# A two-layer metaformer on one core: folds of corners and experts written as additions, and another order of loads at the head of the spectral stage

## The chip, the cores and the metric

The kernel runs on one core of a Trainium2 chip, in float32 throughout. The metric is the device time of one execution in microseconds (us). The engines are named as in the profile: PE (TensorE, matmuls), DVE (VectorE), ACT (ScalarE), POOL (GpSimd), and SP, whose queue issues most DMAs. "L1103" is line 1103 of the kernel before.

## What is computed

The input is 8 images of 128 channels and 32 x 32 tokens. Two layers follow each other:

```
layer 0:  x = x + attention(ln_channels(x))            # 8 heads, all 1024 tokens
          t = t + STU(ln(t))                           # 4 lengths T, T/2, T/4, T/8
   STU:   sum over 16 filters k: causal_conv(phi_k, u) * sigma_k^0.25 @ M_plus_k
          + the same with alternating signs @ M_minus_k, + 3 lags of u @ M_u
layer 1:  x = x + deform(ln_channels(x))               # 3 taps
   deform: offset, mask = convolutions of x with 3 taps, plus their biases
          every tap: 4 bilinear corners (gathered) * weights * mask, @ conv_w
          t = t + experts(ln(t))                       # 8 experts, top 2, gates normalized
   experts: sum over e of gate_e * (t @ expert_w_e) + bias
```

Where the change works, two sums are meant: over 3 taps x 4 corners = 12 gathered rows of 128 channels for each token, added to the token itself; and over 8 experts' gated outputs of 128 channels, added to the token as well.

## The kernel before

**Stages.** Attention runs from the start to about 910 us. Then `spectral_and_second_layer` (from L1533) goes over `work`, 8 images x 16 filters, n = 0 to 127. One n has two halves (`src`), each about 5.19 us of PE: `filter_image` makes the filter's products (p_x, p_y, p_z, L1488) and combines them (ACT L1499 and L1500, POOL's addition L1501, DVE's L1506, L1509, L1516), and `mix` (L1453) multiplies the results of n - 2 with the matrices mf of that filter. `manual_schedule` keeps the order of instructions on each engine as the code writes it.

**The second layer beside it.** While image b is filtered, the second layer of image b - 1 runs in pieces. Two queues of generators, `rows`, are drained by `advance(RATE)`, twice in each half: every `yield` hands back a cost, and pieces are taken until the costs come up to RATE = 3.2 (LAST_RATE = 3.6 while image 7 is filtered, that is for the second layer of image 6). So the costs, which are written by hand, set where an instruction of the second layer stands in its engine's queue. The second layer of image 7 has nothing beside it: from 2558 us it runs alone as the tail (`alone` is true there).

**Corners.** `sampled` (L1052) fetches by 24 indirect DMAs per image (L1077, on POOL), one for each of the NT = 8 groups of 128 tokens and each of 3 taps, into tiles g of 128 x 3 x 4 x 128 (three buffers). ACT scales taps 0 and 1 by the corners' weights (L1095), DVE tap 2 (L1099). Then

```python
nc.vector.tensor_reduce(
    x3[:, i, :], g.rearrange("p t k c -> p c (t k)"), AX.X, ALU.add
)
nc.vector.tensor_add(x3[:, i, :], x3[:, i, :], tok[:, i, :])
```

folds the 12 rows (L1103) and adds the token (L1106). After the eighth group come the statistics (L788, L789), the inverse deviation (L770 to L778; its Newton steps run on POOL while the STU runs, on DVE in the tail), the normalization (L795) and its transposition on PE (p_turn, L919).

**Experts.** For every group PE makes p_e for 4 experts at a time (L1123); ACT gates the first four (L1130), DVE the others (L1135); L1140 folds the 8 rows into a tile `both` by tensor_reduce, and L1143 adds it to x3. PE transposes the sum (p_out, L1155) and it is stored.

**Other work on POOL.** `differences` of the next filter (L1239, L1240), L1501 once per half, and in the first image the sum and difference of the matrices (`terms`, L1371 and L1372).

**The head of the STU.** In this order SP's queue gets: the loads of filters 1 and 2 (`load_filter`, L1257 and L1258, tile teto, three buffers), the four loads of `load_lags` (mu, L1322), the two of `load_parts(0)` (tile m_room, L1366: M_plus and M_minus of filter 0). `prepare(0)` (L1391), an indirect DMA on POOL, is written ahead of them. Once the first half runs, `between` calls `terms` on m_room and loads the next m_room, and in the second half `weigh` (L1379, L1381) makes mf[0], which the first `mix` needs. m_room has one buffer, its tag ("x2") shared with a later tile. Beside it `setup` (from L820) loads the second layer's small weights in pieces, among them the biases of the offsets and masks (L846, L849), zeroes the borders of the tables (L870), and at its end adds the biases to `base` (L906).

Of the kernel before, what the change touches and what calls it, by code (L numbers as in the profile page):

```python
# [11 lines left out]
F32 = mybir.dt.float32  # L12
I32 = mybir.dt.int32
AF = mybir.ActivationFunctionType
ALU = mybir.AluOpType
AX = mybir.AxisListType
PSUM = bass.MemoryType.PSUM

P = 128
B = 8  # L20
C = 128
T = 1024
NT = T // P
# [779 lines left out]
class DeformAndExperts:  # L803
# [17 lines left out]
    def setup(self):  # L821

        nc, cp, ident, dram = self.nc, self.cp, self.ident, self.dram
        (
            conv_w, conv_b, off_w, off_b, mask_w, mask_b, router_w, router_b, expert_w, expert_b
        ) = self.given


        self.gw = cp.tile([C, TAPS * C + TAPS * 9], F32, name="gw")
        nc.sync.dma_start(self.gw[:, 0 : TAPS * C], conv_w.rearrange("c t o -> c (t o)"))  # L830
        off_r = off_w.rearrange("c t (j two) -> c t two j", two=2)
        off_rb = off_b.rearrange("(j two) -> two j", two=2)

        self.base = cp.tile([P, NT, 9], F32, name="base")
        bias = cp.tile([P, 9], F32, name="bias")
        with nc.allow_non_contiguous_dma(reason="small weights"):
            for tap in range(TAPS):
                at = TAPS * C + 9 * tap
                for xy in range(2):
                    nc.sync.dma_start(  # L840
                        self.gw[:, at + 3 * xy : at + 3 * xy + 3], off_r[:, tap, xy, :]
                    )
                nc.sync.dma_start(self.gw[:, at + 6 : at + 9], mask_w[:, tap, :])
                yield
            for xy in range(2):
                nc.sync.dma_start(  # L846
                    bias[:, 3 * xy : 3 * xy + 3], off_rb[xy].partition_broadcast(P)
                )
            nc.sync.dma_start(bias[:, 6:9], mask_b.partition_broadcast(P))  # L849
        yield  # L850
        nc.gpsimd.memset(self.base, 0.0)
        for g in range(4):
            rows = slice(32 * g, 32 * g + 32)
            nc.gpsimd.iota(self.base[rows, :, 0:3], pattern=[[4, NT], [0, 3]], base=g,
                           channel_multiplier=0, allow_small_or_imprecise_dtypes=True)
            nc.gpsimd.iota(self.base[rows, :, 3:6], pattern=[[0, NT], [1, 3]], base=-1,
                           channel_multiplier=1, allow_small_or_imprecise_dtypes=True)

        self.row = cp.tile([P, NT, TAPS], F32, name="row")
        nc.gpsimd.iota(self.row, pattern=[[0, NT], [self.ROWS, TAPS]], base=33,  # L860
                       channel_multiplier=0, allow_small_or_imprecise_dtypes=True)

        zero = cp.tile([33, 4 * C], F32, name="zero")
        nc.gpsimd.memset(zero, 0.0)
        self.tabs = []
        for n in range(2):
            tab = dram.tile([TAPS, self.ROWS, 4, C], F32, name=f"tab{n}")
            for tap in range(TAPS):
                for r0 in (0, T):
                    nc.sync.dma_start(  # L870
                        tab[tap, r0 : r0 + 33].rearrange("r s c -> r (s c)"), zero
                    )
                yield
            self.tabs.append(tab)

        self.shift = [None, ident, None]
        for tap, edge in ((0, 0), (2, 31)):
            s = cp.tile([P, P], F32, name=f"shift{tap}")
            nc.gpsimd.memset(s, 0.0)
            nc.gpsimd.affine_select(  # L880
                out=s, in_=s, pattern=[[-1, P]], base=1 - tap, channel_multiplier=1,
                compare_op=ALU.not_equal, fill=1.0,
            )
            nc.gpsimd.memset(s.rearrange("p (a b) -> p a b", b=32)[:, :, edge : edge + 1], 0.0)
            self.shift[tap] = s
            yield
        self.cb = cp.tile([P, C], F32, name="cb")
        nc.sync.dma_start(self.cb, conv_b.partition_broadcast(P))
        self.rw = cp.tile([C, NE], F32, name="rw")
        nc.sync.dma_start(self.rw, router_w)  # L890
        self.rb = cp.tile([P, NE], F32, name="rb")
        nc.sync.dma_start(self.rb, router_b.partition_broadcast(P))
        yield
        self.ew = cp.tile([C, NE, C], F32, name="ew")
        nc.sync.dma_start(self.ew, expert_w.rearrange("e d c -> d e c"))


        self.ebm = cp.tile([P, NT, C], F32, name="ebm")
        nc.gpsimd.memset(self.ebm, 0.0)
        for i in range(NT):  # L900
            nc.sync.dma_start(self.ebm[i * NE : (i + 1) * NE, i, :], expert_b)
            yield
        self.eidx = cp.tile([P, NT, NE], F32, name="eidx")
        nc.gpsimd.iota(self.eidx, pattern=[[0, NT], [1, NE]], base=0, channel_multiplier=0,
                       allow_small_or_imprecise_dtypes=True)
        nc.vector.tensor_tensor(  # L906
            self.base, self.base, bias.unsqueeze(1).to_broadcast([P, NT, 9]), ALU.add
        )
        yield

# [145 lines left out]
    def sampled(self, b, got, alone):  # L1056
# [3 lines left out]
        nc, sb = self.nc, self.sb  # L1060
        newton = nc.vector if alone else nc.gpsimd
        idx, w, tok = got
        x3 = sb.tile([P, NT, C], F32, tag="x3", name="x3")
# [26 lines left out]
        for i, tap in points:  # L1090
            fetch()
            g = tiles[i]
            if tap < TAPS - 1:
                for k in range(4):
                    nc.scalar.activation(  # L1095
                        g[:, tap, k, :], g[:, tap, k, :], AF.Identity, scale=w[:, i, tap, k : k + 1]
                    )
            else:
                nc.vector.tensor_tensor(  # L1099
                    g[:, tap], g[:, tap], w[:, i, tap, :].unsqueeze(2).to_broadcast([P, 4, C]),  # L1100
                    ALU.mult,
                )
                nc.vector.tensor_reduce(  # L1103
                    x3[:, i, :], g.rearrange("p t k c -> p c (t k)"), AX.X, ALU.add
                )
                nc.vector.tensor_add(x3[:, i, :], x3[:, i, :], tok[:, i, :])  # L1106
            yield 1.7 if alone else 2.6
        tt = sb.tile([P, NT, C], F32, tag="ht", name="tt")
        yield from norm_steps(nc, sb, x3, tt, 1e-5, newton, not alone)
# [8 lines left out]
        for i in range(NT):  # L1118
            g = sb.tile([P, TAPS, 4, C], F32, tag="g", name="ge", bufs=3)
            part = g.rearrange("p t k c -> p (t k) c")[:, 0:NE]  # L1120
            for grp in range(2):
                pe = self.bank("p_e")
                nc.tensor.matmul(  # L1123
                    pe, tc[:, i * P : (i + 1) * P],
                    self.ew[:, grp * 4 : grp * 4 + 4, :].rearrange("d e c -> d (e c)"),
                    start=True, stop=True,
                )
                if grp == 0:
                    for k in range(4):
                        nc.scalar.activation(  # L1130
                            part[:, k], pe[:, k * C : (k + 1) * C], AF.Identity,
                            scale=gate[:, i, k : k + 1],
                        )
                else:
                    nc.vector.tensor_tensor(  # L1135
                        part[:, 4:8], pe.rearrange("p (k c) -> p k c", c=C),
                        gate[:, i, 4:8].unsqueeze(2).to_broadcast([P, 4, C]), ALU.mult,
                    )
                    both = sb.tile([P, C], F32, tag="both", name="both")
                    nc.vector.tensor_reduce(  # L1140
                        both, part.rearrange("p e c -> p c e"), AX.X, ALU.add
                    )
                    nc.vector.tensor_add(x3[:, i, :], x3[:, i, :], both)  # L1143
                yield 1.3 if alone else 2.2
            if i % 4 == 3:
                if not alone:
# [11 lines left out]
                nc.scalar.copy(ot[:, half * 512 : half * 512 + 512], po)  # L1158
                yield
        nc.sync.dma_start(self.out[b].rearrange("c h w -> c (h w)"), ot)  # L1160

    def turn_back(self, src, dst):

# [368 lines left out]

def spectral_and_second_layer(tc, spec, layer, weights):  # L1533
    work = [(b, k) for b in range(B) for k in range(NF)]
    imgs = {0: spec.prepare(0)}
    filters = {0: spec.given.filter, 1: spec.load_filter(1), 2: spec.load_filter(2)}
    less = {0: spec.given.given.diff}
    spec.load_lags()

    mf = {}  # L1540
    parts = spec.load_parts(0)
    both = None

# [44 lines left out]
    for n in range(len(work) + 2):  # L1590
        now = work[n] if n < len(work) else None
        if now is not None:
            b, k = now
            if k == 1 and b + 1 < B:
                starts[b + 1] = spec.begin(b + 1, layer.bank, imgs)
                rows[0].append(starts[b + 1])
            elif k == 0 and b:
                for _ in starts[b]:
                    pass
            us = sums[n] = spec.sb.tile([C, 2, 2, HT], F32, tag="us", name="us", bufs=3)  # L1600
# [128 lines left out]
```

## Time and profile before

| | us |
|---|---|
| median of 3 runs | 2700.72 (2695.61 to 2702.18) |
| the profiled execution | 2699.79 |
| its span (first to last instruction) | 2698.0 |
| busy in it: PE / DVE / POOL / ACT | 2530.0 / 1852.9 / 1448.6 / 1083.5 |
| L1103, 64 folds of corners | 180.4 (2.819 each) |
| L1140, 64 folds of experts | 122.8 (1.919 each) |
| mean granted PE clock | 0.974 of full speed |

A row of the profile gives the line, the engine, the operation, the tiles and shapes, and how often it ran; after the bar come its busy time and the mean of one (in ns), then the idle time of the engine just before it and the instruction that ended that idle time ("<-"). The timeline rows have the start in us, the duration in us and the same names. A row of waits tells who waited for whom: the total in us, how often, and the longest. The 40 digits of a row of slices are the busy tenths of equal parts of the span, 67 us each. In a table of windows the columns are the window, its length, the busy times of PE, PEld (weight loads), DVE, ACT and POOL with the number of instructions, the granted clock, the share of the DMA engines and the GB/s.

### The profile page before, as it was taken

What the parts mean: (1) busy time and instruction counts of PE and PEld (TensorE: products, weight loads), DVE (VectorE), ACT (ScalarE), POOL (GpSimd) and SP (SyncE); (2) the same over time, 40 slices, a digit from 0 to 9 for tenths busy, and PEclk for the clock granted to TensorE, in tenths of its full rate; (3) what the DMA queues carried; (4) which work ended last, traced back from release to release, by engine and by line L of the source; (5) the groups of instructions that cost most, each with busy time, mean ns of one, the idle gap of its engine ahead of it and who ended that gap; (6) DMA issues with size and microseconds to landing.
All of it is one profiled execution on the core that took longest, in us unless ns stands there. A gap on an engine that the chain in (4) does not pass through costs nothing. (4 is left out here: it accounts for less than half of the span.)

```text
span 2698.0 us, 47432 instructions
## 1 busy us (share of the span) xinstructions
PE 2530.0 (94%) x18896; PEld 1769.3 (66%) x18896; DVE 1852.9 (69%) x2728; ACT 1083.5 (40%) x2030; POOL 1448.6 (54%) x1535
## 2 busy tenths in 40 slices
PE   6999999999999799999999999999999999999924
PEld 3555555555555578777787787778778778777712
DVE  3888888888888455448648649648648657658646
ACT  4666766667667111123223224224214224224232
POOL 4777777777788455446246237237236227226230
PEclk9999999999999899999999999999999999999956
DMA  1000000000000254375275266265266266256151
GB/s 29 2 17 2 17 17 2 17 9 10 9 17 17 83 162 153 119 207 160 73 212 169 71 198 184 71 191 176 79 181 194 71 173 194 79 149 202 40 168 35
DMA packets 204675, 267.10 MB, mean 99 GB/s; under 512 B 20308, under 2 KB 138260, under 8 KB 204448
## 3 DMA queue, kind: packets, MB, share of 16 engines
q1 hardware_dynamic: 181312, 205.27, 26.1%
q0 software_dynamic: 16800, 55.59, 6.2%
q10 hardware_dynamic: 6336, 3.15, 0.4%
q8 instruction: 151, 2.47, 0.4%
q14 instruction: 76, 0.62, 0.1%
HBM read 196.02 MB, written 67.92 MB: 98 GB/s over the span
## 5 line engine op out<-in xcount | busy, mean ns | idle before, releaser
L623 POOL TENSOR_TENSOR t<-e 128x1024 f32<-128x1024 f32 x256 | 608.3, 2376 | 199.3 <-ACT e L614 199.0
L651 DVE TENSOR_TENSOR e<-e,rb 128x2048 f32<-128x2048 f32 x256 | 570.8, 2278 | 84.1 <-PE rb L644 84.1
L614 ACT ACTIVATE e<-s 128x2048 f32<-128x2048 f32 x256 | 481.2, 1880 | 253.2 <-PE s L609 250.7
L1501 POOL TENSOR_TENSOR part<-us,part 128x256 f32<-128x256 f32 x256 | 189.9, 743 | 708.5 <-ACT part L1500 707.8
L1453 PE MATMUL po<-us,mf 128*128 128x128 f32 (+2 forms) x2048 | 528.9, 381 | 5.9 <-DVE mf L1381 3.8
L1506 DVE TENSOR_TENSOR part<-p_y,part 128x512 f32<-128x512 f32 x256 | 175.4, 685 | 310.0 <-PE p_y L1488 193.2
L1499 ACT COPY us<-p_x 128x256 f32<-128x256 f32 x256 | 94.8, 370 | 723.2 <-PE p_x L1488 712.8
L1453 PEld LDWEIGHTS po<-us,mf 128*128 128x128 f32 x2048 | 308.2, 191 | 37.5 <-issue 4.8
L609 PE MATMUL s<-q,k 32*128 32x256 f32 x4096 | 296.1, 403 | 14.5 <-ACT e L614 13.7
L661 PE MATMUL av<-e,vt 128*32 128x256 f32 x4096 | 287.9, 388 | 5.3 <-DVE e L651 4.0
L1516 DVE TENSOR_TENSOR us<-p_z,part 128x512 f32<-128x512 f32 x256 | 174.8, 683 | 151.7 <-PE p_z L1488 151.3
L1488 PEld LDWEIGHTS p_z<-diff,gap 128*128 128x128 f32 x1024 | 193.1, 191 | 129.6 <-issue 88.3
L609 PEld LDWEIGHTS s<-q,k 32*128 32x128 f32 x4096 | 186.4, 185 | 137.5 <-ACT e L614 116.3
L1488 PE MATMUL p_z<-diff,gap 128*128 128x256 f32 x1024 | 266.1, 382 | 3.6 <-DVE base L906 3.1
L1095 ACT ACTIVATE g<-g,w 128x128 f32<-128x128 f32 x512 | 161.2, 393 | 118.1 <-DMA g<-tab,here 91.1
L1077 POOL DMA_INDIRECT g<-tab,here x168 | 167.3, 996 | 71.8 <-issue 31.6
L661 PEld LDWEIGHTS av<-e,vt 128*32 128x32 f32 x4096 | 101.3, 109 | 142.2 <-issue 84.3
L1103 DVE TENSOR_REDUCE x<-g 128x128 f32<-128x1536 f32 x64 | 180.4, 2819 | 7.5 <-ACT g L1095 1.5
L1239 POOL TENSOR_TENSOR diff<-teto 128x516 f32<-128x516 f32 x127 | 163.6, 1288 | 1.6 <-DMA teto<-in_phi_o 0.8
L637 DVE RECIPROCAL r<-z 128x256 f32<-128x256 f32 x64 | 112.5, 1757 | 69.5 <-PE z L630 69.3
L1488 PE MATMUL p_y<-diff,gap 128*128 128x256 f32 x512 | 152.6, 379 | 0.1
L1488 PE MATMUL p_z<-teto,ht 128*128 128x256 f32 x512 | 132.3, 381 | 0.0
(264 smaller groups left out, 3731.9 us busy)
## 6 DMA issues: line engine op xcount, KB each, us to landing
mf<-mfd SPq DMA_DIRECT2D x112, 512.0 KB
tab<-gs SPq DMA_DIRECT2D x180, 256.0 KB
teto<-in_phi_o SPq DMA_DIRECT2D x127, 256.5 KB
teto<-in_phi_e SPq DMA_DIRECT2D x127, 256.0 KB
mfd<-mf SPq DMA_DIRECT2D x16, 512.0 KB
xc<-in_x SPq DMA_DIRECT2D x8, 512.0 KB
x1d<-xt SPq DMA_DIRECT2D x8, 512.0 KB
m_room<-in_M_plus SPq DMA_DIRECT2D x16, 256.0 KB
```

Source lines behind the costliest of these rows:

```text
L609: nc.tensor.matmul(s[:, j, c, :], img["k"][rows, hg, 2 * r + c, :], q[rows, qc * QU : (qc + 1) * QU], start=True, stop=True,)
L614: nc.scalar.activation(e.rearrange("p j c q -> p (j c q)"), s.rearrange("p j c q -> p (j c q)"), AF.Exp, scale=float(HD) ** -0.5,)
L623: nc.gpsimd.tensor_add(t, e[:, :, 0, :], e[:, :, 1, :])
L651: nc.vector.tensor_tensor(e, e, un["rb"].unsqueeze(2).to_broadcast([P, NH, 2, QU]), ALU.mult)
L661: nc.tensor.matmul(qrt["av"][32 * j : 32 * j + 32, 0:QU], img["v"][:, 2 * r + c, P * hg + 32 * j : P * hg + 32 * j + 32], un["e", r][:, j, ...
L1077: nc.gpsimd.indirect_dma_start(out=tiles[-1][:, tap].rearrange("p k c -> p (k c)"), out_offset=None, in_=rows, in_offset=bass.IndirectOffs ...
L1103: nc.vector.tensor_reduce(x3[:, i, :], g.rearrange("p t k c -> p c (t k)"), AX.X, ALU.add)
L1453: self.nc.tensor.matmul(out, lhsT, rhs, start=bank not in img["opened"], stop=last, skip_group_check=True)
L1488: nc.tensor.matmul(out, weights, moving, start=start, stop=stop, skip_group_check=True)
L1501: nc.gpsimd.tensor_add(part[:, 0], mine[:, :, 0:P], part[:, 1])
L1506: nc.vector.tensor_tensor(part[:, 2:4], y[:, 0].unsqueeze(1).to_broadcast([C, 2, 2, P]), part[:, 0:2], ALU.add)
L1516: nc.vector.tensor_tensor(result(2, 4), z, part[:, 2:4], ALU.add)
```

## The change

The two folds are written as chains of additions. `add_up(g, (6, 3))` adds rows 6 to 11 of the 12 to rows 0 to 5 (768 elements per partition), then rows 3 to 5 to rows 0 to 2 (384); `three` adds the first of the three left to the token, and the other two to that sum (128 elements each). For the experts `add_up(part, (4, 2))` has 512 and 256 elements, and two additions of 128 go straight into x3; the tile `both` of that place is gone. All their operands are in SBUF. At the head, `load_parts(0)` comes first, then filter 1, `prepare(0)`, `load_lags`, and filter 2. The addition of the biases leaves `setup` for a generator of its own, `settle`, that is queued when filter 1 of image 0 begins; the loads of the biases stay where they were.

```diff
@@ setup
-        nc.vector.tensor_tensor(
-            self.base, self.base, bias.unsqueeze(1).to_broadcast([P, NT, 9]), ALU.add
+        yield
+
+    def settle(self):
+        yield
+        self.nc.vector.tensor_tensor(
+            self.base, self.base, self.bias.unsqueeze(1).to_broadcast([P, NT, 9]), ALU.add
         )
         yield
@@ sampled
-                nc.vector.tensor_reduce(
-                    x3[:, i, :], g.rearrange("p t k c -> p c (t k)"), AX.X, ALU.add
-                )
-                nc.vector.tensor_add(x3[:, i, :], x3[:, i, :], tok[:, i, :])
+                self.add_up(g.rearrange("p t k c -> p (t k) c"), (6, 3))
+                self.three(x3[:, i, :], g[:, 0, 0:3], tok[:, i, :])
...
-                    both = sb.tile([P, C], F32, tag="both", name="both")
-                    nc.vector.tensor_reduce(
-                        both, part.rearrange("p e c -> p c e"), AX.X, ALU.add
-                    )
-                    nc.vector.tensor_add(x3[:, i, :], x3[:, i, :], both)
+                    self.add_up(part, (4, 2))
+                    for k in range(2):
+                        nc.vector.tensor_add(x3[:, i, :], x3[:, i, :], part[:, k])
...
+    def add_up(self, parts, counts):
+        for n in counts:
+            self.nc.vector.tensor_add(parts[:, 0:n], parts[:, 0:n], parts[:, n : 2 * n])
+
+    def three(self, out, parts, more):
+        self.nc.vector.tensor_add(out, parts[:, 0], more)
+        for k in (1, 2):
+            self.nc.vector.tensor_add(out, out, parts[:, k])
@@ spectral_and_second_layer
-    imgs = {0: spec.prepare(0)}
-    filters = {0: spec.given.filter, 1: spec.load_filter(1), 2: spec.load_filter(2)}
-    less = {0: spec.given.given.diff}
-    spec.load_lags()
 
     mf = {}
     parts = spec.load_parts(0)
     both = None
+    filters = {0: spec.given.filter, 1: spec.load_filter(1)}
+    less = {0: spec.given.given.diff}
+    imgs = {0: spec.prepare(0)}
+    spec.load_lags()
+    filters[2] = spec.load_filter(2)
...
                 rows[0].append(starts[b + 1])
+                if b == 0:
+                    rows[0].append(layer.settle())
```

More of the change, by code (lines that the diff above doesn't have):

```diff
@@ L834, in setup @@
         self.base = cp.tile([P, NT, 9], F32, name="base")
-        bias = cp.tile([P, 9], F32, name="bias")
+        bias = self.bias = cp.tile([P, 9], F32, name="bias")
         with nc.allow_non_contiguous_dma(reason="small weights"):
```

## The prediction, on record ahead of the run

> **What bounds the kernel now.** I read the span in slices first, then busy times of single stages, the waits of the STU, and last single rows. The slices (each 67 us):
>
> ```profile
> PE   6999999999999799999999999999999999999924
> DVE  3888888888888455448648649648648657658646
> POOL 4777777777788455446246237237236227226230
> ```
>
> From slice 14 (the STU, 913 to 2558 us) PE is full; DVE and POOL rise together once per image, when the second layer gathers its corners. Only the last two slices leave PE idle. So an edit on DVE pays in three places: the tail, the head, and where DVE holds PE up. One gather stage (image 0's, us; columns PE, PEld, DVE, ACT, POOL):
>
> ```profile
> 1206.00:1257.00 51.00, 50.35 (x237) 40.86 (x237) 46.21 (x52) 23.94 (x81) 38.93 (x43) 1.00 0.65 192
> ```
>
> DVE is busy 46.2 of 51 us. POOL is busy 38.9 in 43 instructions, and the trace shows 0.30 us between its gathers, so it is nearly full as well. Who releases PE, and whom POOL holds up, between 970 and 2560:
>
> ```profile
> PE p_turn L919 <- DVE tt L795: 10.1, 18, 1.0
> PE po L1453 <- DVE us L1516: 2.1, 1, 2.1
> PE p_back L1168 <- DVE x L1530: 1.6, 1, 1.6
> DVE part L1506 <- POOL part L1501: 84.4, 28, 6.2
> ```
>
> PE waits little, but mostly for L795, the normalization that follows the corners. That is where a late fold would come through. Next the rows of the folds and of the one two-input DVE operation beside them:
>
> ```profile
> L1103 DVE TENSOR_REDUCE x<-g 128x128 f32<-128x1536 f32 x64 | 180.4, 2819 | 7.5 <-ACT g L1095 1.5 <-issue 0.5
> L1140 DVE TENSOR_REDUCE both<-ge 128x128 f32<-128x1024 f32 x64 | 122.8, 1919 | 6.2
> L1099 DVE TENSOR_TENSOR g<-g,w 128x512 f32<-128x512 f32 x64 | 54.6, 854 | 14.7 <-DMA g<-tab,cn_idx 12.6 <-DMA g<-tab,here 2.0
> L1106 DVE TENSOR_TENSOR x<-x,tok 128x128 f32<-128x128 f32 x64 | 30.4, 474 | 2.3
> ```
>
> In the tail, alone, L1099 takes 0.69 and L1106 0.29 us: means of 0.854 and 0.474 mean stretching in the STU. Why, at 1233 us:
>
> ```profile
> 1233.61 1.29 POOL L1239 TENSOR_TENSOR diff<-teto 128x516 f32<-128x516 f32 x1
> 1233.73 1.78 DVE L1099 TENSOR_TENSOR g<-g,w 128x512 f32<-128x512 f32 x1 [0.69 <-DMA g<-tab,here]
> 1234.85 1.25 POOL L1240 TENSOR_TENSOR diff<-teto 128x258 f32<-128x258 f32 x1
> ```
>
> L1099 starts beside L1239 and ends about when that has ended plus its own 0.6; then L1240 (0.77 on average) takes 1.25 because it waits for L1099. The two don't overlap. L1103 shows nothing of it: 2.82 on average, 2.75 alone.
>
> [...] the gather issue at 2612.62, inside an L1099, took 1.41 for 0.96. [...] Here, already after the 2.06 us stall at 2479.7, rows of 1.02 took 1.81, 1.91 and 1.23: 1.88 us more.
>
> **The change, part by part.** Prices: 768 elements 0.955, 384 0.555, 512 0.69, 256 0.42, 128 0.29, plus 0.03 for a dependent step, 0.21 for a start-to-start of the last.
>
> *A fold alone.* Corner: 2.79 + 0.21 = 3.00 goes, 0.985 + 0.585 + 0.31 + 0.31 + 0.21 = 2.40 comes: -0.60. Expert: 1.95 + 0.21 = 2.16 goes, 0.72 + 0.45 + 0.31 + 0.21 = 1.69 comes: about -0.45. [...]
>
> *Tail, nothing beside DVE but gathers.* (a) At 2562 DVE works off image 6's last two expert folds before L788 of image 7: -0.9. (b) Corners: DVE's period is 3.79, but POOL issues three gathers at 0.96 + 0.30 each, 3.79 too. A faster DVE gains at most the last fold, -0.6. [...] +2 to +4 over 24 by stepping them through, against 0.6 now. Sum +1.8 (-0.7 to +3). (c) Experts: DVE's period 2.95 (0.69+1.92+0.29 and gaps) is above PE's 2.1, so 8 x -0.45 = -3.6. **Tail -2.7** (-5.1 to -1).
>
> *Head.* SP now issues m_room(0) at 920.3 behind teto1, teto2 and mu; it lands for POOL at 927.21 and PE waits for the first matrices:
>
> ```profile
> 933.92 2.08 PE L1453 MATMUL po<-us,mf 128*128 128x128 f32 x6 [3.80 <-DVE mf L1381]
> 940.91 1.27 POOL L1371 TENSOR_TENSOR both<-m_room 128x512 f32<-128x512 f32 x1 [9.84 <-DMA m_room<-in_M_minus]
> 945.29 1.13 PE L1407 MATMUL p_ut<-flip,ht 128*128 128x128 f32 x8 [2.55 <-DVE us L1509]
> ```
>
> With m_room(0) first on SP (two DMAs ahead of teto1, four mu, teto2's two), terms(0) can start at 922.5 and the 3.80, and about 1.9 of low clock after it, go. But m_room(1) stays behind setup's small loads, at 932.05 on SP, and lands at 940.9; POOL's L1501, DVE's L1509 and PE's p_ut hang on it, and so does a 3.08 wait at 951.6. It moves only if SP starts earlier: 0 to 2.5 us. PE's gain becomes a longer wait at p_ut. teto2 moves behind mu, needed later: nothing. The indirect load of prepare runs on POOL's queue, which is not late: nothing. **Head -1.5** (0 to -3; -15 if every stall and its low clock fell).
>
> *Biases.* The base add (0.22 us of DVE) moves from setup's end to filter 1; its loads stay. First use is more than 100 us later. 0, at most +0.2 if DVE isn't hidden.
>
> *Expert folds in the STU, images 0 to 6.* DVE has slack and PE doesn't wait for them, except at 2356 (1.58 for L1530, and 1.7 of low clock): -1 (0 to -3). L1143 shows only 0.08 of stretch.
>
> *Corner folds in the STU.* This decides. In image 0's stage (50 us) POOL's three additions take 6.5 + 4.3 + 7.3 = 18.1 us. DVE's locking instructions now cover 8 x 0.98 = 7.8 us, 16% of it, so 0.16 x 18.1 = 2.9 us should be waited: measured 2.2 here and, over the 56 folds of the STU, (54.6 + 30.4 - 64 x 0.98)/56 = 0.40 each, 3.2 an image. The rule holds. After, they cover 8 x (0.69 + 0.08 + 2.40) = 25.4 us, 51%: 9.2 us waited, 6 to 7 more, against a saving of 8 x 0.60 = 4.8. So +1.2 to +2.2, and more because gathers fall into the lock too: I take +2.5 an image (-1 to +6). After the last fold DVE runs back to back through L788/L789 into L770, POOL's Newton steps and L795, for which PE already waits; later passes through in full, earlier gains only those 10.1 us in seven images at most. A wait of 1.4 + 2.5 comes near the stall that halved the clock: I add 1.0 (0 to 1.9). **Six images x 3.5 = +21.** Image 6 advances faster (3.6 for 3.2) and DVE is 8 us behind already, with the 2.06 + 1.88 stall: contention and saving there, 0 (-3.9 to +6).
>
> **Sum**: -2.7 - 1.5 - 1 + 21 + 0 = +16 on the profiled execution's 2699.8 us (span 2698.0, 1.8 around it; 0.9 below the median 2700.72). That gives 2716, +0.6%.
>
> **Rivals.** *Savings win (faster).* The lock costs less than the additions save. Place: the corner stages. Price: contention stays under 4.8 us an image more, i.e. under 3.2 + 4.8 = 8 of the 18.1 us wait (44% instead of 51%). From there DVE is earlier, image 6's stall falls (-3.9), 2356 gives -3, the tail -5.1, the head -1.5: -13.5, 2686. For it: 51% is near 44%, and short additions leave openings to POOL. Against: POOL's own waits add up too. *Nothing reaches PE.* PE's queue absorbs both: tail, head and 2356 alone, -5.2, 2694.6. For it: PE waits 10 us in 1600. *POOL becomes the bound.* Gathers and additions queue behind DVE's chain, and the stage is paced by POOL: of its 40 instructions in the stage 51% start inside a lock and wait the rest of it, 0.32 us on average for these lengths, 6.5 an image, with 1.9 of clock 8.4, x 6 = +50 - 5: 2745. For it: POOL's 38.9 us plus gaps already fill the stage.
>
> **How the numbers follow.** Forecast (main, about 2702 to 2732) 0.45; savings win 0.25; nothing reaches PE 0.18; POOL the bound 0.12. Range 2686 to 2740: it leaves out about half of the first rival and half of the last, 0.19 together. A measurement of this kernel tells 0.3% (8.1 us) from no change. Faster than that: 0.24 + 0.05 = 0.29. Slower: 0.35 of the main case + 0.12 = 0.47. Within: the rest, 0.24.
>
> **What would show it.** L1103 and L1140 replaced by additions; in the STU the 768-element one well above 0.955 us on average and the 128s near 0.5; L1239, L1240, L1501 and gathers longer; p_turn's wait for L795 well above 10.1 us. In the tail a gather spacing above 1.265, and expert periods near 2.5. In the head, no 3.80 at L1381 and a p_ut wait of about 5 or more. Wrong if these additions run near their uncontended times in the STU, or p_turn's wait doesn't grow, or m_room(1) lands before 936.

## The result, and the profile after

The changed kernel took 2711.34 us (median of 6 runs, 2705.53 to 2712.31) against 2701.45 (6 runs): ratio 1.0036, 95% interval 1.0021 to 1.0051, so 6 to 14 us slower. The forecast was 2716 within 2686 to 2740. The profiled execution took 2705.53 us, its span is 2703.7, 5.7 more than the span of before.

In the changed kernel L1166 is `add_up` (768, 384, 512 and 256 elements), L1170 and L1172 are `three`, L1144 the last additions of the experts. Older lines have moved: L1099 is L1104, L1077 L1082, L1239/L1240 L1251/L1252, L1501 L1513, L1506/L1509/L1516 L1518/L1521/L1528, L1453 L1465, L919 L924, L1168 L1180, L1381 L1393, L1407 L1419, L1488 L1500, L1529/L1530 L1541/L1542. L927 is ACT's copy of half of p_turn's result into tc.

The first gather stage in the table of windows, and the waits of the STU (970 to 2560), as shown of before:

```profile
1206.00:1257.00 51.00, 49.29 (x225) 39.56 (x224) 47.51 (x83) 20.99 (x70) 37.48 (x38) 1.00 0.65 192
```

```profile
PE p_turn L924 <- DVE tt L795: 10.7, 16, 1.0
PE po L1465 <- DVE us L1521: 7.6, 6, 1.3
PE p_back L1180 <- ACT x L1541: 4.9, 7, 0.7
PE p_turn L924 <- ACT tc L927: 3.7, 5, 0.8
PE p_back L1180 <- DVE x L1542: 1.6, 1, 1.6
```

PE has lost 1.06 us of busy time in this stretch. A new wait has come, six times 1.3 us: `mix` waits for L1521, an addition of the filter itself. p_turn waits longer as well: with the 3.7 us put down to L927, a row that before doesn't have, 14.4 us for 10.1, some 0.6 an image. The groups of DVE in the STU, by shape (1000 to 2565):

```profile
L1166 DVE TENSOR_TENSOR g<-g 128x768 f32<-128x768 f32 x56 | 94.8, 1693 | 6.4 <-ACT g L1100 1.4
L1104 DVE TENSOR_TENSOR g<-g,w 128x512 f32<-128x512 f32 x56 | 46.7, 834 | 0.5 <-DMA g<-tab,here 0.5
L1166 DVE TENSOR_TENSOR g<-g 128x384 f32<-128x384 f32 x56 | 40.4, 721 | 1.9
L1172 DVE TENSOR_TENSOR x<-x,g 128x128 f32<-128x128 f32 x112 | 35.2, 314 | 3.8
L1170 DVE TENSOR_TENSOR x<-g,tok 128x128 f32<-128x128 f32 x56 | 27.2, 485 | 1.9
```

Against the tail of the same execution (0.959, 0.692, 0.557, 0.292 and 0.292 us for the same five shapes) the excess of a corner is 0.73 + 0.14 + 0.16 + 0.04 + 0.19 = 1.28 us; before it was 0.40. The means hide how it falls: in each of images 0 to 5 the 768-element addition of the second and of the fifth corner takes 3.5 to 3.6 us, beside L1251, L1252 and L1513 in a row, and the seventh corner's L1170 takes 1.94. The other 768-element ones take 0.96 to 1.39 there, the other L1170 0.29. What it looks like, in the timeline around the seventh corner of image 0:

```profile
1243.58 1.04 POOL L1513 TENSOR_TENSOR part<-us,part 128x256 f32<-128x256 f32 x1
1244.07 1.94 DVE L1170 TENSOR_TENSOR x<-g,tok 128x128 f32<-128x128 f32 x1
1244.59 1.27 POOL L1251 TENSOR_TENSOR diff<-teto 128x516 f32<-128x516 f32 x1
1245.82 0.77 POOL L1252 TENSOR_TENSOR diff<-teto 128x258 f32<-128x258 f32 x1
1246.04 1.03 DVE L1172 TENSOR_TENSOR x<-x,g 128x128 f32<-128x128 f32 x2
1246.99 0.68 DVE L1518 TENSOR_TENSOR part<-p_y,part 128x512 f32<-128x512 f32 x1
1247.59 0.41 DVE L1521 TENSOR_TENSOR us<-p_y,part 128x256 f32<-128x256 f32 x1
1248.06 0.70 PE L1465 MATMUL po<-us,mf 128*128 128x256 f32 x2 [1.25 <-DVE us L1521]
```

An addition of 128 elements takes 1.94 us: it is recorded from 1244.07, when POOL's L1513 is under way (to 1244.62), and ends at 1246.01, just after L1251 too is done (1245.86). The next, L1172, then waits for L1252: 1.03 us for two that take 0.62 alone. L1518 and L1521 stand behind it on DVE, and PE waits for L1521.

The head, where before PE waited 3.80 for mf, 2.55 at p_ut and 3.08 at p_z:

```profile
929.26 1.15 PE L1465 MATMUL po<-us,mf 128*128 128x128 f32 x6 [1.48 <-DVE mf L1393]
942.39 2.05 PE L1419 MATMUL p_ut<-flip,ht 128*128 128x128 f32 x8 [5.90 <-DVE us L1521]
948.67 1.10 PE L1500 MATMUL p_z<-diff,gap 128*128 128x256 f32 x4 [1.50 <-DVE us L1521]
```

9.43 us of stalls have become 8.88: most of what the first and the third gain is given back at the second. The head as a whole is 2.4 us shorter (table below); 1.8 of that is PE's own busy time there (51.8 to 50.0 us), not these stalls.

PE runs the same 18,896 matmuls in the same order in both traces, so the nth of one can be laid against the nth of the other. The differences of their start times:

| stretch (times of before) | after minus before, us | the prediction's term |
|---|---|---|
| up to PE's first matmul of the STU (913.5), not touched | -3.5 | 0 |
| head, to 975 | -2.4 | -1.5 |
| images 0 to 5 beside the STU: +1.6, +3.8, +2.4, +3.8, +2.8, +2.4 | +16.8 | +21 |
| around 2356 | -1.9 | -1 |
| image 6 | +0.2 | 0 |
| hand-over to the tail | -0.4 | -0.9 |
| tail, to the experts | +2.1 | +1.8 |
| tail, experts | -5.1 | -3.6 |
| sum | +5.8 | +16 |

Without the first row, attention's own scatter, the change comes to +9.2, near the +9.9 of the medians. The terms hold the chance of the clock as well: 3.4 of the +16.8 are two stretches at half clock (images 1 and 3) that before doesn't have, and the -1.9 around 2356 is one that only before has.

### The profile page after: what moved, and what is told of

It reads as the page before. It is cut to its first block, busy times and chain, and to the rows that moved or that the text cites. A ratio compares the mean times of both kernels' runs of the same rounds, so it can differ in the third digit from the quotient of the medians.

```text
span 2703.7 us, 47771 instructions
## 1 busy us (share of the span) xinstructions
PE 2528.0 (94%) x18896; PEld 1768.9 (65%) x18896; DVE 1830.4 (68%) x3048; ACT 1083.5 (40%) x2030; POOL 1478.7 (55%) x1535
## 3 DMA queue, kind: packets, MB, share of 16 engines
q10 hardware_dynamic: 6336, 3.15, 0.4%
## 5 line engine op out<-in xcount | busy, mean ns | idle before, releaser
L1513 POOL TENSOR_TENSOR part<-us,part 128x256 f32<-128x256 f32 x256 | 200.9, 786 | 697.8 <-ACT part L1512 697.3
L1465 PE MATMUL po<-us,mf 128*128 128x128 f32 (+2 forms) x2048 | 529.7, 381 | 10.3 <-DVE us L1521 7.6
L1518 DVE TENSOR_TENSOR part<-p_y,part 128x512 f32<-128x512 f32 x256 | 175.6, 686 | 316.9 <-PE p_y L1500 197.2
L1465 PEld LDWEIGHTS po<-us,mf 128*128 128x128 f32 x2048 | 307.9, 191 | 45.3 <-DVE us L1521 8.7
L1528 DVE TENSOR_TENSOR us<-p_z,part 128x512 f32<-128x512 f32 x256 | 175.1, 684 | 154.8 <-PE p_z L1500 154.5
L1500 PEld LDWEIGHTS p_z<-diff,gap 128*128 128x128 f32 x1024 | 192.1, 190 | 127.8 <-issue 92.6
L1500 PE MATMUL p_z<-diff,gap 128*128 128x256 f32 x1024 | 265.1, 381 | 3.1 <-DVE us L1521 3.0
L1082 POOL DMA_INDIRECT g<-tab,here x168 | 179.2, 1067 | 70.1 <-issue 27.7
L1251 POOL TENSOR_TENSOR diff<-teto 128x516 f32<-128x516 f32 x127 | 163.3, 1286 | 4.8 <-DMA teto<-in_phi_o 4.0
L1166 DVE TENSOR_TENSOR g<-g 128x768 f32<-128x768 f32 (+1 forms) x128 | 147.3, 1151 | 9.3 <-ACT g L1100 1.4
L1500 PE MATMUL p_y<-diff,gap 128*128 128x256 f32 x512 | 152.7, 379 | 0.0
L1500 PE MATMUL p_z<-teto,ht 128*128 128x256 f32 x512 | 132.4, 381 | 0.0
```

The costliest lines, as they stand in the source:

```text
L1082: nc.gpsimd.indirect_dma_start(out=tiles[-1][:, tap].rearrange("p k c -> p (k c)"), out_offset=None, in_=rows, in_offset=bass.IndirectOffs ...
L1251: lambda: nc.gpsimd.tensor_sub(blocks[:, :, 0:2], pair, one),
L1465: self.nc.tensor.matmul(out, lhsT, rhs, start=bank not in img["opened"], stop=last, skip_group_check=True)
L1500: nc.tensor.matmul(out, weights, moving, start=start, stop=stop, skip_group_check=True)
L1513: nc.gpsimd.tensor_add(part[:, 0], mine[:, :, 0:P], part[:, 1])
L1518: nc.vector.tensor_tensor(part[:, 2:4], y[:, 0].unsqueeze(1).to_broadcast([C, 2, 2, P]), part[:, 0:2], ALU.add)
```

## Experiments

**What the runs say together.** "STU" is the time between the same two PE matmuls (975 and 2545 us in before) in the profiled execution; "half clock" is how long the trace shows PE's clock at 0.5 in it. It comes in stretches of 3.4 us (3.41 from 2357 of before), each worth about 1.7, so one profile more or less of them must not be taken for an effect. Runs marked with a star leave part of the computation out.

| kernel | median, us | ratio to before (95%) | corners in the STU | STU, us | half clock |
|---|---|---|---|---|---|
| before | 2701.23 to 2701.57 in five sets | 1 | reduce | 1570.0 | 10.2 |
| head_only | 2700.43 | 0.9995 (0.9985 to 1.0006) | reduce | 1573.2 | 17.1 |
| corners_reduced | 2696.04 | 0.9974 (0.9965 to 0.9982) | reduce | 1568.9 | 13.7 |
| after | 2711.34 | 1.0036 (1.0021 to 1.0051) | add | 1585.1 | 13.7 |
| corners_only | 2715.00 | 1.0050 (1.0032 to 1.0068) | add | 1585.9 | 13.7 |
| fold_in_two | 2721.04 | 1.0069 (1.0052 to 1.0085) | add, cut | 1599.3 | 17.1 |
| unlocked_reduce * | 2677.34 | 0.9910 (0.9893 to 0.9926) | reduce | 1556.6 | 3.4 |
| unlocked_adds * | 2669.41 | 0.9882 (0.9866 to 0.9898) | add | 1550.2 | 3.4 |
| unlocked_two * | 2673.10 | 0.9897 (0.9880 to 0.9914) | add, cut | 1554.9 | 0.0 |
| setup_later | 2688.37 | 0.9957 (0.9944 to 0.9971) | reduce | 1566.8 | 6.8 |
| tail_adds | 2686.74 | 0.9949 (0.9932 to 0.9967) | reduce | 1566.7 | 6.8 |
| act_scales | 2661.10 | 0.9848 (0.9832 to 0.9864) | reduce | 1547.3 | 3.4 |
| act_scales_adds | 2683.26 | 0.9932 (0.9919 to 0.9946) | add | 1566.9 | 3.4 |

**Which part loses.** *head_only* takes the kernel before with the new head and `settle` only.

> The kernel before with the head's new order and the later biases alone; both folds stay tensor_reduce. By the aligned traces the head gave about -3.6 us between PE's start in the STU and 975 us. Theory (the folds make the loss, the head gains): -3.6, some 2697 to 2698, ratio 0.9987; PE's wait for the first matrices near 1.5 us, for p_ut near 5.9. Rival (the head's order shifts later work, and part of the loss is its own): no faster than before.

-1.4 us by the ratio, interval -4 to +2. Its three stalls (1.93, 5.80, 1.72) come to 9.45 us, those of before to 9.43. The -3.6 expected was read from one pair of profiles (from a slightly later matmul than the -2.4 of the table) and was partly clock: corners_only, whose head is that of before, also went through it 4.2 us faster than before did, with 5.0 us at half clock in place of 13.4. The interval holds -3.6, the recorded term (-1.5) and zero; the rival, a loss, isn't seen.

*corners_reduced* is the changed kernel with

```diff
-                self.add_up(g.rearrange("p t k c -> p (t k) c"), (6, 3))
-                self.three(x3[:, i, :], g[:, 0, 0:3], tok[:, i, :])
+                nc.vector.tensor_reduce(
+                    x3[:, i, :], g.rearrange("p t k c -> p c (t k)"), AX.X, ALU.add
+                )
+                nc.vector.tensor_add(x3[:, i, :], x3[:, i, :], tok[:, i, :])
```

> The changed kernel with the corners folded by tensor_reduce again; experts by additions, head as changed. Theory (the corner additions lose 17 us in the STU and 2.5 in the tail, all else gains): head -3.6, the wait at 2356 -1.8, the tail's hand-over -0.8 and its experts -5: about -11 against before, 2690, ratio 0.996; no waits of 1.3 us of PE's mix for L1521. Rival (the expert additions lose in the STU as well, [...]): -3 or less.

-7.0 us (-5 to -9): between the two expectations, and faster than before. PE's wait for L1521 at the mix is gone. The rival isn't seen: beside the STU the experts' additions take nearly what they take in the tail (512 elements 0.694 for 0.693 us, 256 0.440 for 0.425, 128 0.310 for 0.292). *corners_only* makes the opposite edit on the kernel before.

> The kernel before with the corners' additions alone; experts and head as before. Theory: +17 in the STU's first six images, about 0 in image 6, +2.5 in the tail: +17 to +21, some 2720, ratio 1.007; the 768-element addition 1.7 us on average in the STU and 0.96 in the tail. Rival (the loss needs the experts' or the head's change too): under +10.

+13.5 us (+9 to +18): less than the theory's +17 to +21, more than the rival's +10, with an interval that reaches into both. The corner additions cost 0.0050 by this pair and 0.0062 by the other (1.0036 less 0.9974), 13 to 17 us; the rest of the change gains about 7. The 768-element addition took 1.646 us on average in the STU.

**Is it POOL's reading?** What the recorded texts call a lock is what 1233 us of before shows: beside each other, DVE's L1099 took 1.78 us for 0.69 and POOL's L1240 1.25 for 0.77. In the two next runs POOL's additions of the STU are memsets of like length, which write and don't read:

```diff
-        for make in filter_differences(self.nc, t, d):
-            make()
+        for n in (DIFFS, DIFFS, 600):
+            self.nc.gpsimd.memset(d[:, 0:n], 0.0)
...
-        nc.gpsimd.tensor_add(part[:, 0], mine[:, :, 0:P], part[:, 1])
+        nc.gpsimd.memset(part[:, 0:2], 0.0)
+        nc.gpsimd.memset(part[:, 0], 0.0)
```

> The kernel of the run corners_reduced in which POOL's additions of the STU (differences of the filters, and L1513) are memsets of about the same length (0.8 + 0.8 + 0.6, and 0.5 + 0.3 us): POOL stays as busy, but reads no SBUF in them. It leaves those sums out of the computation. It is the base for the next run; expected within 5 us of corners_reduced.

> The changed kernel with the same memsets in place of POOL's additions (those sums are left out). Theory (DVE's two-input additions and POOL's reads of SBUF shut each other out): the 768-element addition falls from 1.69 to about 0.96 us in the STU, L1170 from 0.49 to 0.29, and the kernel is no longer slower than the run unlocked_reduce in the STU, +3 at most in all for the tail's gathers. Rival 1 (five dependent instructions cost more than one, whoever is beside them): +17 to +19 against unlocked_reduce as it is with the additions. Rival 2 (the lock covers POOL's writes and its gathers as much as its reads): additions still stretched well above 1.2 us.

The sign turns: adds are 0.0028 (8 us) faster than reduce (2668.69 to 2669.80 us against 2675.18 to 2678.66, measured together), where with POOL's additions they are 0.0062 slower. The same five groups in unlocked_adds:

```profile
L1166 DVE TENSOR_TENSOR g<-g 128x768 f32<-128x768 f32 x56 | 53.7, 959 | 6.2 <-ACT g L1100 0.9 <-issue 0.4
L1104 DVE TENSOR_TENSOR g<-g,w 128x512 f32<-128x512 f32 x56 | 39.1, 699 | 5.0 <-DMA g<-tab,here 5.0
L1166 DVE TENSOR_TENSOR g<-g 128x384 f32<-128x384 f32 x56 | 34.2, 610 | 1.9
L1172 DVE TENSOR_TENSOR x<-x,g 128x128 f32<-128x128 f32 x112 | 32.7, 292 | 3.8
L1170 DVE TENSOR_TENSOR x<-g,tok 128x128 f32<-128x128 f32 x56 | 16.3, 292 | 1.9
```

0.959 for 1.693 and 0.292 for 0.485, beside a POOL that issues as many gathers and is as busy (755.8 us in the STU, for 742.1 in the changed kernel); only the 384-element one keeps 0.05. So the stretch goes with POOL's additions, which read SBUF, and neither with its being busy nor with its writing; rivals 1 and 2 are out. The first expectation missed: unlocked_reduce is 17 us faster than corners_reduced by the ratios, not within 5. Read in the same way, POOL cost PE time already before the change, by what the two operations with two SBUF inputs beside the old fold, L1099 and L1106 (0.876 and 0.500 us in the STU, 0.696 and 0.292 in the tail), and others like them waited for it; that is inferred, and which of them cost how much wasn't tried one by one.

**Can the chain be placed better?** *fold_in_two* cuts it:

```diff
-                self.add_up(g.rearrange("p t k c -> p (t k) c"), (6, 3))
+                self.add_up(g.rearrange("p t k c -> p (t k) c"), (6,))
+                if not alone:
+                    yield 1.3
+                self.add_up(g.rearrange("p t k c -> p (t k) c"), (3,))
                 self.three(x3[:, i, :], g[:, 0, 0:3], tok[:, i, :])
-            yield 1.7 if alone else 2.6
+            yield 1.7 if alone else 2.6 if tap < TAPS - 1 else 1.3
```

> The changed kernel with the corners' chain cut in two in the STU: after the 768-element addition a yield of 1.3 (the yield after the fold is 1.3 in place of 2.6), so that the filter's DVE operations can stand between the pieces. Theory A (PE loses because the filter's L1521 is queued behind the whole chain at the seventh corner): the six stalls of 1.4 us go, up to -8 against the changed kernel. Theory B (DVE's lateness is what counts, wherever it comes out): the stalls at the mix go and p_turn's wait for L795 grows by as much; within 2 us of the changed kernel.

Both theories missed: 9 us slower than the changed kernel by the ratios. The excess of a corner grew from 1.28 to 1.71 us (L1104 0.765, then 1.698, 0.718, 0.511, and twice 0.552). PE's waits for the filter's addition (L1521 of the changed kernel, L1524 here) grew from 9.1 to 19.2 us, and p_turn's stayed (14.8 for 14.4). From its timeline (here L1173 is the first of `three`, L1254 and L1255 the differences, L1516 POOL's addition for the filter, and L1521 is L1518 of the changed kernel):

```profile
1238.97 3.15 DVE L1173 TENSOR_TENSOR x<-g,tok 128x128 f32<-128x128 f32 x1
1239.32 1.29 POOL L1254 TENSOR_TENSOR diff<-teto 128x516 f32<-128x516 f32 x1
1240.56 0.73 POOL L1255 TENSOR_TENSOR diff<-teto 128x258 f32<-128x258 f32 x1
1241.25 0.72 POOL L1516 TENSOR_TENSOR part<-us,part 128x256 f32<-128x256 f32 x1
1242.16 0.62 DVE L1175 TENSOR_TENSOR x<-x,g 128x128 f32<-128x128 f32 x2
1242.69 0.68 DVE L1521 TENSOR_TENSOR part<-p_y,part 128x512 f32<-128x512 f32 x1
```

A 0.29 us addition takes 3.15, until three of POOL's in a row are done, with the filter's L1521 behind it. Its record begins 0.35 us ahead of the first of the three; why it doesn't go first isn't shown. *unlocked_two* asks whether that is all, by the memsets of above in this kernel.

> The run fold_in_two (the corners' chain cut in two) with POOL's additions of the STU replaced by memsets, as in unlocked_adds (those sums are left out). Fold_in_two was 9 us slower than the changed kernel. Theory (cutting the chain gives POOL more openings to take the lock, and the second piece waits again): without POOL's reads nothing is lost, within 3 us of unlocked_adds or faster. Rival (the new places of DVE's instructions delay PE by themselves): slower than unlocked_adds by most of the 9 to 12 us here too.

It isn't: 4 us slower than unlocked_adds by the ratios, whose intervals overlap (the runs themselves don't: 2672.53 to 2674.39 against 2668.69 to 2669.80). Taken as it stands, some 4 of the 9 us come from the new places alone and the other 5 with POOL's additions. Neither expectation holds in full.

**The other terms.** *setup_later* tests whether the head's later stalls hang on m_room(1) behind setup's small loads:

```diff
-    rows = [deque([spec.channels(imgs[0], layer.bank), layer.setup()]), deque()]
+    rows = [deque([spec.channels(imgs[0], layer.bank)]), deque()]
...
                 parts = spec.load_parts(1)
+                rows[0].append(layer.setup())
                 return
```

> The run corners_reduced, with the second layer's setup queued only after the load of m_room(1), so that SP issues that load some 8 us earlier. Theory (the two later stalls of the head hang on m_room(1) behind setup's small loads): p_ut's wait of 5.9 us and the 1.5 after it mostly go, with their low clock: -5 to -9 against corners_reduced. Rival (setup's loads then delay what comes next, the following m_room or filter): within 2 us of it.

4.6 us faster than corners_reduced by the ratios (0.9957 for 0.9974), just short of the -5 to -9 expected. PE's waits between 905 and 975 (L1467 is `mix` here, L1395 `weigh`, L1502 the filter's products); before, after, head_only and corners_reduced all show 9 us in three stalls there:

```profile
PE po L1467 <- DVE mf L1395: 2.0, 1, 2.0
PE p_x L1502 <- DMA teto<-in_phi_o: 1.1, 1, 1.1
PE av L661 <- DVE e L651: 1.1, 1, 1.1
```

p_ut and p_z no longer wait; the head (913.5 to 975) took 51.6 us for 59.2. *tail_adds* puts the corners' additions into setup_later's tail alone.

> The run setup_later, with the corners' additions in the tail alone (image 7), tensor_reduce in the STU. The prediction put them at +1.8 there (-0.7 to +3), because gathers that start inside a two-input addition are late. Theory: gather spacing in the tail 1.40 us on average against 1.31, the corner stage +1 to +2 against setup_later. Rival (nothing is late, the last fold is shorter): -0.6.

The gathers come later: spacing 1.382 for 1.304 us. The last corner is folded 38.95 us after the first gather for 38.17, and PE goes on from there 0.7 us later, between the two expectations. The tail as a whole is as long within 0.2, for the experts' stage, the same code in both, was 0.9 shorter; the runs can't be told apart (0.9949 and 0.9957). Over all thirteen profiles the time from first gather to last fold is 38.2 on average with reduce and 38.5 with additions. In before and after it was 37.4 and 39.5, the two ends of the scatter.

**A kernel that beats both.** If operations that POOL's additions stretch cost PE in the gather stage, taking L1099 (0.876 us for 0.696) away must gain. ACT, 24 of 51 us busy in that stage, can scale the third tap too:

```diff
-            if tap < TAPS - 1:
+            if tap < TAPS - 1 or not alone:
                 for k in range(4):
                     nc.scalar.activation(
...
+            if tap == TAPS - 1:
                 nc.vector.tensor_reduce(
```

> The run setup_later, but in the STU ACT scales all three taps, so that L1099's DVE multiplication, the longest instruction with two SBUF inputs left in the corner stage, is gone there (in the tail it stays). Theory (what locking DVE does in that stage costs PE, beside its own time): DVE loses 8 x 0.69 us of work and most of 0.17 us of waiting each per image, PE's waits of the gather stages shrink: -3 to -10 against setup_later. Rival (ACT's queue now delays L1500, on which POOL's L1501 and DVE's L1506 hang, and the tap's scaling comes later than DVE's): same or slower than setup_later.

29 us faster than setup_later by the ratios (27 by the medians), 41 (37 to 45) faster than before: far more than expected. p_turn's waits for the corners' normalization, 21 times and 11.7 us in setup_later, no longer appear, and the STU is 19.5 us shorter. How much of that is the stretch and how much the 0.69 us of work isn't told apart by this run. *act_scales_adds* has the additions again on top.

> The run act_scales with the corners folded by additions again (STU and tail). ACT does the scaling, so DVE has 5.5 us more room per image. Theory (the chain waits for POOL's additions, 1.3 us a corner, whatever stands before it, and DVE's room takes part of it): slower than act_scales, by +3 to +14, less than the 17 us that the same edit cost beside L1099. Rival (the loss needed a DVE that is full; with room the shorter fold wins): same or faster than act_scales.

22 us slower than act_scales: in the theory's direction but outside its range; DVE's room doesn't soften the loss. The corner's excess is 1.22 us for 0.29 (L1112 there: 0.582), 0.93 more against 0.60 saved, over 56 corners 18.5 us; the STU grew by 19.6.

## Why the prediction was right, and where its sizes were off

**The prices.** Those for 768, 384 and 256 elements (0.955, 0.555, 0.42) are estimates: the line through two rows of before, 0.69 us at 512 and 0.29 at 128 elements, gives 0.957, 0.557 and 0.423. Measured in the tail of the changed kernel: 0.959, 0.557 and 0.425, and 0.693 and 0.292 for the other two.

**The corner folds in the STU: right, 21 for 16.8.** The author's rule (DVE's time in operations with two SBUF inputs as a share of the stage, times POOL's additions) gave 9.2 us of waiting an image; 8 x 1.28 = 10.2 was measured. The growth, "6 to 7 more", was 7.0, and 4.8 was saved, so DVE is 2.25 later and PE, over six images, 2.8, of which 0.6 is clock. That the waits are for POOL's additions is shown by the runs with memsets in their place: the 768-element addition falls from 1.693 to 0.959 us, and DVE's additions win by 8 us. How the waits fall was not foreseen: the rule spreads them evenly over the stage, but the same two corners of every image bear about half of them. That a share of time still gave the sum may be luck in part: the rule was not tried on another pattern.

**The way to PE: half wrong.** The step "back to back through L788/L789 into L770, POOL's Newton steps and L795, for which PE already waits; later passes through in full" named the wrong first place. 1.3 us of each image comes earlier, at the mix, because the filter's own L1521 is queued on DVE behind the stretched chain; p_turn's wait for L795, which was to come out "well above 10.1 us", hardly grew (10.7), and with the wait put down to L927 by some 0.6 an image. I had followed the second layer's data and not asked what else stands in DVE's queue.

**The half clock: 1.0 an image was too much.** Images 1 and 3 show it (rows of 634 ns for 379, 1.7 us lost each), but before had it in image 4; over images 0 to 5 three stretches for one, 0.6 an image.

**The head: right in kind, its size not settled.** The first stall went from 3.80 to 1.48, not to nothing, for filter 1's load stood behind m_room and POOL waited 4.0 us for it ahead of `terms`; p_ut took 5.90, as foreseen. head_only's -1.4 (-4 to +2) agrees with -1.5 and with nothing, and its stalls are no shorter in sum than those of before. setup_later shows what held the rest.

**Tail.** Experts: 8 x 0.45 = 3.6 was forecast; 3.2 to 5.1 came in the ten profiles with additions there, laid against before; DVE's period fell from 2.95 to 2.51, as said. Corners: +1.8 was probably too much. The issues that begin inside one of DVE's two-input operations are late, in after 13 of 23 with 1.24 us for 0.96, in before 6 with 1.06; in sum as stepped through (3.7 us over 24 for 0.6), but of that tail_adds shows 0.7 on PE's path and the thirteen profiles 0.3, within a scatter of 2.

**The biases** (`settle`): 0.22 us of DVE at 949, nobody waits; before, p_z was released only by L906, at most 0.2 us later. **At 2356: wrong, and near in size by luck.** The expert additions were to end PE's wait for L1530 (1.58 us). It is 1.55 to 1.58 us in all ten kernels that keep POOL's additions, whichever way the experts are folded, and 1.14 in the three with memsets. In the changed kernel the two first additions of that fold take 1.58 us for the 0.69 + 0.43 of the tail, beside POOL's L1251 and L1252: POOL takes back there what the shorter fold gives. What went is the half clock after the stall, 3.41 us of it, which makes the -1.9; it follows this stall in seven of the thirteen profiles, with either fold.

**The sum** is too high by 6 us: 4 from the corner folds, 1 to 1.5 each from the head, 2356 and the experts (where clock and scatter are as large as the terms), and 1 the other way from image 6 and the tail's first part. Savings win needed less than 8 of 18.1 us waited, and 10.2 were. POOL as the bound would have lost 8.4 an image, clock included, and 2.8 was lost: POOL waits less than DVE does. In the STU its gather issues went from 0.996 to 1.067 us, L1501's additions from 0.742 to 0.788 and L1240's from 0.772 to 0.787; L1239's, which were to be longer too, did not change (1.288 and 1.286). Nothing reaches PE fell with the waits at L1521.

## What to carry to other kernels

Before a tensor_reduce is replaced by shorter additions, look at what GpSimd does at that moment: an addition with both inputs in SBUF can be held by GpSimd's additions, by several in a row (here 0.96 us became 3.5 to 3.6 through three), and can hold them (L1252: 1.18 us for 0.74 at 2363), so price it with the stretched rows of a two-input operation that already runs there, not with its time alone. Such an edit can pay in one stage and lose in another; here experts' folds gain in the tail and corners' lose beside the spectral stage. And follow lateness down the engine's own queue: the first to suffer here was what is issued behind the late instruction (`mix`, by way of L1521, six times 1.3 us), not the next step of its data (p_turn, some 0.6 an image).

## What the runs showed of the hardware that was not expected

- Waiting need not alternate. Twelve times in the changed kernel a DVE addition of 0.96 us took 3.5 to 3.6, through three GpSimd additions in a row, though its record begins 0.04 to 0.16 us before the first of them. At 1233 us of before, DVE's L1099 did come between two of GpSimd's. What decides isn't shown.
- A two-input DVE operation also holds up GpSimd's gather issues. In the tails of all thirteen profiles, the first gather of each left aside, 132 issues begin inside such an operation and take 1.15 us on average; the other 167 take 0.955, none over 0.97.
- GpSimd memsets of the same length beside the same additions cost these almost nothing (768 elements: 0.959 us in both the STU and the tail).
- Four ACT operations of 0.39 us in place of one DVE multiplication of 0.69 made the kernel 27 to 29 us faster.
